# Gate and up of a second MLP by halves of the tokens, with seven matmuls in place of eight inside each product

## The chip, the cores and the metric

The kernel runs on one core of a Trainium2 chip. The core has a matrix engine (PE, with its weight loads, PEld), three engines for elementwise work (DVE, ACT, POOL) and a queue, SP, that issues all DMA transfers here. The engines run side by side, each through its own list of instructions in order, and wait for one another by semaphores. Matmul results go to PSUM[...]. The metric is the device time of one launch in microseconds, lower is better; differences are judged on the median.

## The reference

```python
x = x + 0.5 * ffn(layernorm(x))     # first MLP
x = x + attention(layernorm(x))     # 16 heads of 32, causal
x = x + 0.5 * ffn(layernorm(x))     # second MLP, same weights
# ffn:  inter = gelu(x @ Wg.T) * (x @ Wu.T);  out = inter @ Wd.T
```

x is 2048 tokens by 512 in float32. Wg and Wu are 4096 by 512, Wd is 512 by 4096; they come as 4-bit codes with scales. The first MLP decodes them and stores the decoded blocks in device memory; the second reads them back. All is float32.

## The kernel before

Both MLPs run in the function `ffn`. The 4096 inner rows are taken in 8 groups of 512, each in two halves (h = 0, 1) of 256. The 2048 tokens are two pairs of blocks (tp = 0, 1), 1024 tokens each. For a given group, h and tp, `slot` multiplies a 256 by 512 weight block by 512 by 1024 activations, for gate and then for up, in Strassen's way: each side is cut into 2 by 2 blocks, and seven products of sums of blocks stand for the eight products of blocks. A product is two matmuls of 128 by 128 weights with 512 columns (`product`, L313), which add in one PSUM bank. Each of the seven results is read out of PSUM once, by ACT (L352, L364) or DVE (L355 to L373), and the results are added up on the way; a sum of two results that both lie in SBUF is left to POOL (L367). ACT then does the gelu, in place (L333), and DVE the product of gate and up (L337), which gives `inter`.

The weight sums lie stored with the weights (made by the first MLP on POOL, L269 to L272). The token sums are made once, by `token_sums` (L293 to L296): for the first pair ahead of the first slot, t3 on POOL, for the second pair inside the first group.

The down projection (`down_pieces`) is in Strassen's form too: four sums of blocks of inter (L397 to L400, on DVE in the second MLP), then 14 pieces, each four matmuls of 256 columns (L412). Pieces read their bank by DVE (L420) or ACT (L434) into the residual x, and POOL adds intermediate results (L426). The 14 pieces of one tp are put one by one between the products of a later slot, so PE has other work while a bank is being read.

The program's order is written out by hand: each engine's instructions stand in the order in which this code emits them. The second MLP's first weights are fetched during the attention's sixth pass (`next_w`, L945), and the tokens of its first two blocks are normalized and transposed during the last pass. Blocks 2 and 3 are normalized inside the second MLP's first group. Later weights come as one transfer of 1792 KB for each half group, two buffers in turn, and wd as one transfer for each group (L539). PSUM has a pool of seven banks, `ps_one`, handed out in turn. The functions that the change touches, as the profile numbers their lines:

Of the kernel before, what the change touches and what calls it, by code (L numbers as in the profile page):

```python
# [2 lines left out]

# [6 lines left out]
F32 = mybir.dt.float32  # L10
# [4 lines left out]
AF = mybir.ActivationFunctionType  # L15
ALU = mybir.AluOpType
AX = mybir.AxisListType

P = 128
S = 2048  # L20
D = 512
H = 16
HD = 32
NT = S // P
NB = S // 512
NG = 8
NPAIR = H // 2
NQ = H // 4
EPS = 1e-5
# [5 lines left out]
def macaron_kernel(ctx: ExitStack, tc: tile.TileContext, x, packed, scales, wqk, bqk, wv, bv, wo, bo, out):  # L35
# [6 lines left out]
    nc = tc.nc  # L42
    PSUM = bass.MemoryType.PSUM

    const = ctx.enter_context(tc.tile_pool(name="const", bufs=1))
    res = ctx.enter_context(tc.tile_pool(name="res", bufs=1))
    small = ctx.enter_context(tc.tile_pool(name="small", bufs=2))
    store = ctx.enter_context(tc.tile_pool(name="store", bufs=1, space=bass.MemoryType.DRAM))
    ps_one = ctx.enter_context(tc.tile_pool(name="ps_one", bufs=7, space=PSUM))
# [5 lines left out]
    def weights(nm):  # L55
        return wts.tile([P, 7 * 512], F32, tag="w", name=nm)


    xpair = [res.tile([P, 2, D], F32, tag=f"x{t}", name=f"x{t}") for t in range(NT // 2)]
    xs = [xpair[t // 2][:, t % 2, :] for t in range(NT)]  # L60

    def load_x(tb):
# [5 lines left out]
    ident = const.tile([P, P], F32, tag="ident", name="ident")  # L68
    make_identity(nc, ident)
    eps = const.tile([P, 1], F32, tag="eps", name="eps")  # L70
    nc.gpsimd.memset(eps, EPS)
    expo = const.tile([P, 4], F32, tag="expo", name="expo")
    nc.gpsimd.memset(expo, -0.5)

    root = const.tile([P, 1], F32, tag="root", name="root")
# [2 lines left out]
    class Norm:  # L78
# [3 lines left out]
        def __init__(  # L82
            self, phase, tb, t_out, temp, on_act=(0, 1, 2, 3), on_pool=(), moments_on_act=False, power=False
        ):
            nm = f"{phase}_{tb}"
            tiles = [xs[4 * tb + i] for i in range(4)]

            def column(tag):
                return small.tile([P, 4], F32, tag=tag, name=f"{tag}_{nm}")

            rstd, nbias = column("rstd"), column("nbias")
# [27 lines left out]
            def scales():  # L119

                if power:
                    if moments_on_act:
                        nc.gpsimd.tensor_scalar(rstd, square, 1.0 / D, EPS, ALU.mult, ALU.add)
                    else:
                        nc.gpsimd.tensor_scalar(rstd, mv[:, :, 1], EPS, None, ALU.add)
                    nc.gpsimd.tensor_tensor(rstd, rstd, expo, ALU.pow)
                    if moments_on_act:
                        nc.gpsimd.tensor_tensor(nbias, total, rstd, ALU.mult)
                    elif on_act:
                        nc.gpsimd.tensor_scalar(nbias, mv[:, :, 0], -1.0, None, ALU.mult)  # L130
                        nc.gpsimd.tensor_tensor(nbias, nbias, rstd, ALU.mult)
                else:
                    nc.scalar.activation(rstd, mv[:, :, 1], AF.Sqrt, bias=eps)
                    nc.vector.reciprocal(rstd, rstd)
                    if on_act:
                        nc.vector.scalar_tensor_tensor(nbias, mv[:, :, 0], -1.0, rstd, ALU.mult, ALU.mult)
# [41 lines left out]
    def x_transposed(phase, tb):  # L178
        return res.tile([P, 4, 512], F32, tag=f"xT{tb}", name=f"xT_{phase}_{tb}")


    kept = {}

    def ffn(phase, finish, behind, loads, ready=(), first_w=None):
# [8 lines left out]
        with tc.tile_pool(name=f"w{phase}", bufs=1) as wp, tc.tile_pool(name=f"dq{phase}", bufs=1) as dq, tc.tile_pool(  # L193
# [283 lines left out]
            def run(steps):  # L477
                for f in steps:
                    f()
# [87 lines left out]
            for group in groups:  # L567
                run(group)

    def attention(xT, xT_f, wqk_wv, next_w):  # L570
        with tc.tile_pool(name="aw", bufs=1) as aw, tc.tile_pool(name="qk", bufs=1) as qkp, tc.tile_pool(
            name="pp", bufs=3
# [15 lines left out]
                out=mask_f, in_=mask_f, compare_op=ALU.is_ge, fill=MASKED, base=0, pattern=[[-1, P]], channel_multiplier=1  # L588
# [87 lines left out]
            later, divisions = [], {}  # L676
# [235 lines left out]
            qk, v = project_qk(0), project_v(0)  # L912
# [29 lines left out]
            for p in range(NPAIR):  # L942
                if p in refill:
                    nc.sync.dma_start(out=wqk_sb, in_=wqk[refill[p]])
                if p == 5:  # L945
                    next_w()
                fills = plan[p]() if p in plan else [[] for _ in range(NB)]
                if p == 4:
                    for piece in project_v(1)[:2]:
# [21 lines left out]
                n = 0  # L971
                for steps in attend(p, 2 if p + 1 == NPAIR else 1):
# [4 lines left out]
                    other = next(ahead, None)  # L977
# [30 lines left out]
    xT_a, xT_f, early = [], [], {}  # L1008
# [26 lines left out]
        nc.sync.dma_start(out=bv_sb, in_=bv.partition_broadcast(P))  # L1035

    def load_first():
        early["ffn"] = weights("w_2_0_0")
        nc.sync.dma_start(out=early["ffn"], in_=kept[0, 0])

    ffn(1, lambda *_: None, norms_behind, load_qkv)
    attention(xT_a, xT_f, early["qkv"], load_first)

    def store_out(t, half, x_):

        rows = out[t * P : (t + 2) * P, half * 256 : half * 256 + 256]
        nc.sync.dma_start(out=rows.rearrange("(j p) n -> p j n", p=P), in_=x_)

    ffn(2, store_out, lambda temp: [], lambda: None, xT_f, early["ffn"])


# [62 lines left out]
```

## Time and profile before

| | us |
|---|---|
| median of 3 runs | 3267.97 (3267.74 to 3269.58) |
| the profiled execution, its own time | 3267.61 |
| its span, first to last instruction | 3265.8 |
| PE, DVE, POOL, ACT busy | 3236.0, 1887.5, 1130.4, 873.4 |
| second MLP, first matmul to last instruction | 2099.3 to 3265.8 |
| one group of it (2851.18 to 2995.66) | 144.48 |

The span leaves out what lies around the program. A busy share says how long an engine had work, not that the work was needed then. In lists of groups, the columns are line, engine, operation, output and inputs with their shapes, count, then busy us and mean ns of one, then idle time of the engine before them and what ended it. A line's own view gives the shortest, median and longest duration in ns. A timeline line starts with its start and its duration in us. A float32 matmul shows as two PE records, so a product of two 512-column matmuls is four records.

### The profile page before, as it was taken

The numbers are of one execution on the slowest core, as the hardware profiler recorded it, in microseconds if no ns is written. First come the engines' busy times: TensorE is split into PE (matmuls) and PEld (weight loads), VectorE is DVE, ScalarE is ACT, GpSimd is POOL, SyncE is SP. The second block draws the span as 40 slices with busy tenths as digits, with TensorE's granted clock in tenths as the row PEclk, the third lists the DMA queues.
The fourth block names the chain that finished last, engine by engine and source line by source line (L and its number), as shares of the span: only waits on it lengthen the run. The fifth ranks groups of instructions, "written<-read, shape, count | busy, mean of one in ns | idle before, by whom it ended". The sixth has DMA issues, their size and how long they took to land.

```text
span 3265.8 us, 34006 instructions
## 1 busy us (share of the span) xinstructions
PE 3236.0 (99%) x12656; PEld 1720.2 (53%) x12656; DVE 1887.5 (58%) x2918; ACT 873.4 (27%) x1848; POOL 1130.4 (35%) x1339
## 2 busy tenths in 40 slices
PE   7999999999999999999999999999999999999999
PEld 3556565655656565333344333356556565655556
DVE  6666666666666555575654675555455445445545
ACT  4111111111111131464544555531111111111111
POOL 3546364555546341332212223213122221313222
PEclk9999999999999999999999999999999999999999
DMA  4111111111111100000000000101010101101101
GB/s 142 65 71 42 66 71 48 65 65 71 42 65 69 48 17 7 9 12 6 13 5 6 30 19 9 49 23 45 23 68 23 45 23 45 46 23 47 44 23 52
DMA packets 42054, 134.14 MB, mean 41 GB/s; under 512 B 5864, under 2 KB 26344, under 8 KB 35360
## 3 DMA queue, kind: packets, MB, share of 16 engines
q1 hardware_dynamic: 41888, 131.96, 11.0%
q8 instruction: 100, 1.64, 0.2%
q14 instruction: 66, 0.54, 0.1%
HBM read 81.91 MB, written 48.46 MB: 40 GB/s over the span
## 4 chain that ended last, share of the span: by engine, by line
PE 95%; ACT 2%; DVE 1%; POOL 1%; issue 1%; DMA 0%; SPq 0%; POOLq 0%; DVEq 0%; ACTq 0%
PE po L412 24%; PE pu L313 23%; PE pg L313 23%; PE av L779 8%; PE pm L714 6%; PE pqk L625 4%; PE ps L840 2%; PE pv L642 2%; PE pp L664 2%; PE ps L849 1%; ACT pt L872 1%; PE pt_f L153 0%; ACT both L788 0%; DVE parts L729 0%; PE pt_a L153 0%
## 5 line engine op out<-in xcount | busy, mean ns | idle before, releaser
L412 PE MATMUL po<-wd,inter 128*128 128x256 f32 x2048 | 482.2, 379 | 0.0
L313 PE MATMUL pg<-xT_f,w 128*128 128x512 f32 x1024 | 478.0, 595 | 0.4 <-ACT u L352 0.4
L313 PE MATMUL pu<-xT_f,w 128*128 128x512 f32 x1024 | 476.0, 592 | 0.0
L412 PEld LDWEIGHTS po<-wd,inter 128*128 128x128 f32 x2048 | 389.0, 190 | 155.2 <-issue 109.5
L729 DVE TENSOR_REDUCE parts<-pm 128x1 f32<-128x512 f32 (+3 forms) x640 | 370.5, 608 | 149.6 <-PE pm L714 135.6
L367 POOL TENSOR_TENSOR u<-u,u 128x512 f32<-128x512 f32 x128 | 162.9, 1272 | 839.4 <-ACT u L364 839.4
L426 POOL TENSOR_TENSOR x<-x,d 128x512 f32<-128x512 f32 x248 | 323.5, 1315 | 333.2 <-DVE d L420 164.8
L412 PE MATMUL po<-wd,s 128*128 128x256 f32 x1536 | 362.4, 379 | 0.0
L313 PE MATMUL pg<-xsum,w 128*128 128x512 f32 x768 | 356.7, 593 | 0.0
L313 PE MATMUL pu<-xsum,w 128*128 128x512 f32 x768 | 355.3, 592 | 0.0
L412 PEld LDWEIGHTS po<-wd,s 128*128 128x128 f32 x1536 | 291.4, 190 | 116.2 <-issue 82.8
L714 PE MATMUL pm<-kT,qT 32*128 32x512 f32 (+3 forms) x1280 | 334.3, 574 | 0.1
L872 ACT ACTIVATE pt<-ps 128x512 f32<-128x512 f32 (+3 forms) x576 | 271.8, 532 | 130.9 <-PE ps L849 130.0
L779 PE MATMUL av<-pt,vaug 128*64 128x512 f32 (+3 forms) x1280 | 299.7, 552 | 2.8 <-ACT both L788 2.3
L313 PEld LDWEIGHTS pg<-xT_f,w 128*128 128x128 f32 x1024 | 195.2, 191 | 194.3 <-issue 179.4
L313 PEld LDWEIGHTS pu<-xT_f,w 128*128 128x128 f32 x1024 | 194.3, 190 | 191.8 <-issue 183.2
L849 PE MATMUL ps<-qT,kT 32*128 32x512 f32 (+3 forms) x1280 | 277.9, 533 | 0.0
L313 PEld LDWEIGHTS pu<-xsum,w 128*128 128x128 f32 x768 | 145.8, 190 | 144.3 <-issue 139.0
L313 PEld LDWEIGHTS pg<-xsum,w 128*128 128x128 f32 x768 | 145.7, 190 | 142.5 <-issue 137.6
L420 DVE SCALAR_TENSOR_TENSOR d<-po,d 128x512 f32<-128x512 f32 x192 | 132.1, 688 | 107.4 <-PE po L412 106.5
L420 DVE SCALAR_TENSOR_TENSOR x<-po,x 128x512 f32<-128x512 f32 x192 | 131.8, 687 | 102.4 <-ACT d L434 69.7
L866 POOL TENSOR_SCALAR_AFFINE_SELECT pt<-pt 128x256 f32<-128x256 f32 x128 | 52.0, 406 | 396.1 <-ACT pt L865 395.8
(136 smaller groups left out, 3436.0 us busy)
## 6 DMA issues: line engine op xcount, KB each, us to landing
kept<-wd SPq DMA_DIRECT2D x8, 1792.0 KB
wd<-kept SPq DMA_DIRECT2D x8, 1792.0 KB
x<-in_x SPq DMA_DIRECT2D x16, 256.0 KB
pk<-in_gate_codes SPq DMA_DIRECT2D x16, 256.0 KB
sc<-in_gate_scales SPq DMA_DIRECT2D x32, 128.0 KB
pk<-in_up_codes SPq DMA_DIRECT2D x16, 256.0 KB
sc<-in_up_scales SPq DMA_DIRECT2D x32, 128.0 KB
pk<-in_down_codes SPq DMA_DIRECT2D x16, 256.0 KB
```

The costliest lines, as they stand in the source:

```text
L313: nc.tensor.matmul(ps, lhsT=a[:, j, :], rhs=b[:, j, :], start=(j == 0), stop=(j == 1))
L367: nc.gpsimd.tensor_tensor(u4, u4, u2, ALU.add)
L412: nc.tensor.matmul(ps[:, j, :], lhsT=a[i][:, k, bass.ts(2 * q + j, P)], rhs=b[i][:, k, :], start=(k == 0), stop=(k == 1),)
L420: stt(dst, ps, 0.5, other, ALU.mult, ALU.add)
L426: adder.tensor_tensor(dst, dst, other, ALU.add)
L625: nc.tensor.matmul(ps, lhsT=w[:, j, k, :], rhs=xT[tb][:, k, :], start=(k == 0), stop=(k == 3))
L642: nc.tensor.matmul(ps[:, i, :], lhsT=xT[t // 4][:, k, (t % 4) * P : (t % 4 + 1) * P], rhs=wv_sb[:, k, bass.ts(half, 256)], start=(k == 0), ...
L714: nc.tensor.matmul(ps[a][:, :n], lhsT=q[r, bass.ts(4 * g + i, P)], rhs=k[r, kb * 512 : kb * 512 + n], start=True, stop=not on_pe,)
L729: nc.vector.tensor_reduce(parts[:, a, i, kb : kb + 1], ps[a][:, :n], AX.X, ALU.max)
L779: nc.tensor.matmul(av[64 * a : 64 * a + 64, off:], lhsT=vaug[:, c, p % 4, HD * a : HD * a + 2 * HD], rhs=pt[:, a, off:], start=(c == 0), s ...
L849: nc.tensor.matmul(ps[a][:, off:], lhsT=k[r, bass.ts(c, P)], rhs=q[r, g * 512 + off : (g + 1) * 512], start=False, stop=True,)
L872: nc.scalar.activation(pt[:, a, plain:], ps[a][:, plain:], AF.Exp, scale=scale)
```

## The change

The second MLP leaves `ffn` and gets a function of its own, `second_ffn`; the first MLP stays.

- It goes through all eight groups with the first 1024 tokens, and then again with the other 1024. The rows of x of the later tokens are written to device memory (`away`) at its start. They are read back one block of 128 rows at a time for their normalization (the class `Later`: moments in the first half, then normalize on ACT, transpose on PE and copy on ACT around the border of the halves), and once more as the residual after the first half's last stores.
- A *problem* is one of the seven outer products of one group and h, now for gate and up together: 2 by 2 blocks of 128 by 128 weights against 2 by 2 blocks of 128 by 256 tokens. Its eight block products are replaced by seven, again in Strassen's way. Two problems form a *pair*, and share a PSUM bank, half of it each.
- Of the seven inner results some add up in PSUM: bank d takes products 1, 6, 7 and 4 in turn, and is read after each; f takes 5 and 3; e takes 2. ACT does four reads and DVE three (`pair`). The seven outer results are added one pair later, in SBUF (`recombine`): on DVE, and two of seven on POOL.
- The inner weight sums are made on POOL for each pair, two pairs ahead (`weight_sums`), from blocks that SP fetches four pairs ahead. The inner token sums are made on DVE, once in each half (`Tokens.inner`).
- Seven pairs are a group. The 14 down pieces of a group run during the next group's seven pairs, two in each; its four down sums stand in the second of these.
- Step numbers in `hooks` are the products of a pair: what stands at step k is emitted after the k-th.

```diff
-    xpair = [res.tile([P, 2, D], F32, tag=f"x{t}", name=f"x{t}") for t in range(NT // 2)]
+    xquad = [res.tile([P, 4, D], F32, tag=f"xq{t}", name=f"xq{t}") for t in range(NT // 4)]
+    xpair = [xquad[t // 2][:, 2 * (t % 2) : 2 * (t % 2) + 2, :] for t in range(NT // 2)]
...
+    problems = [(g, h, i) for g in range(NG) for h in range(2) for i in (1, 2, 6, 7, 5, 4, 3)]
+    NP = len(problems) // 2
...
+    def pair_of(n):
+        return problems[2 * (n % NP) : 2 * (n % NP) + 2]
...
+    def fetch(slot, pair):
+        for k, (g, h, i) in enumerate(pair):
+            place = {1: 0, 5: 1, 2: 2, 4: 3, 7: 4, 6: 5, 3: 6}[i]
+            nc.sync.dma_start(
+                out=slot[:, k, 0:4, :].rearrange("p (m c) n -> p m (c n)", m=2),
+                in_=kept[g, h].rearrange("p (m i c n) -> p i m (c n)", m=2, i=7, c=2)[:, place],
+            )
+    def weight_sums(slot):
+        a11, a12, a21, a22, s3, s2, s4 = [slot[:, :, y, :] for y in range(7)]
+        eng = nc.gpsimd
+        eng.tensor_tensor(s3, a11, a21, ALU.subtract)
+        eng.tensor_tensor(s2, a22, s3, ALU.subtract)
+        eng.tensor_tensor(a21, a21, a22, ALU.add)
+        eng.tensor_tensor(s4, a12, s2, ALU.subtract)
...
+    def second_ffn(finish, ready, slots):
...
+            away = store.tile([P, 2, 4 * D], F32, tag="away", name="away")
+            for q in range(2):
+                nc.sync.dma_start(out=away[:, q, :], in_=xquad[2 + q].rearrange("p t n -> p (t n)"))
+            residual = [xquad[0], xquad[1]]
...
+                def outer(self, first):
+                    b11, b21, b12, b22, t3, t2, t4 = [self.operand(x) for x in range(7)]
+                    return [
+                        lambda: first.tensor_tensor(t3, b22, b12, ALU.subtract),
+                        lambda: tt(t2, t3, b11, ALU.add),
+                        lambda: tt(b12, b12, b11, ALU.subtract),
+                        lambda: tt(t4, b21, t2, ALU.subtract),
+                    ]
...
+                def inner(self, t):
+                    n = 2 if t < 3 else 1
+                    v = (self.b1, self.b2, self.ts, self.t4)[t][:, : 2 * n, :].rearrange("p (x c) n -> p x c n", c=2)
+                    b11, b21 = [v[:, :, c, :256] for c in range(2)]
+                    b12, b22 = [v[:, :, c, 256:] for c in range(2)]
+                    t3, t2, t4 = [self.ys[:, 2 * t : 2 * t + n, k, :] for k in range(3)]
+                    t1 = b12 if t > 0 else self.t4[:, 2, :].rearrange("p (x n) -> p x n", x=2)
+                    return [
+                        lambda: tt(t3, b22, b12, ALU.subtract),
+                        lambda: tt(t1, b12, b11, ALU.subtract),
+                        lambda: tt(t2, t3, b11, ALU.add),
+                        lambda: tt(t4, b21, t2, ALU.subtract),
+                    ]
...
+            def pair(n, tokens, pieces, hooks):
...
+                fb = [tokens.factors(i) for _, _, i in pair_of(n)]
...
+                def product(ps, y, first=False):
+                    for k in range(2):
+                        nc.tensor.matmul(
+                            ps[:, k, :], lhsT=fa[k][y], rhs=fb[k][y], start=first and k == 0, stop=True,
+                            skip_group_check=True,
...
+                order = (1, 5, 2, 6, "a", 7, 3, "b", 4) if pieces else (1, 5, 6, 2, 7, 3, 4)
+                step = 0
+                for y in order:
+                    if y in ("a", "b"):
+                        for piece in pieces[y == "b"]:
+                            piece()
+                        continue
+                    if y == 1:
+                        d = bank("d")
+                        product(d, 1, True)
+                        u1 = taken("u1")
+                        nc.scalar.copy(u1, d)
+                    elif y == 5:
+                        f = bank("f")
+                        product(f, 5, True)
+                        u5 = taken("u5")
+                        nc.scalar.copy(u5, f)
+                    elif y == 2:
+                        e = bank("e")
+                        product(e, 2, True)
+                        tt(o[:, :, 0, :256], e, u1, ALU.add)
+                    elif y == 6:
+                        product(d, 6)
+                        u2 = taken("u2")
+                        nc.scalar.copy(u2, d)
+                    elif y == 7:
+                        product(d, 7)
+                        tt(o[:, :, 1, 256:], d, u5, ALU.add)
+                    elif y == 3:
+                        product(f, 3)
+                        tt(o[:, :, 0, 256:], f, u2, ALU.add)
+                    else:
+                        product(d, 4)
+                        nc.scalar.copy(o[:, :, 1, :256], d)
+                    for s in hooks.get(step, ()):
+                        s()
+                    step += 1
...
+            def recombine(n):
...
+                for g, h, i in pair_of(n):
+                    o = {j: outs.get((half, g, h, j)) for j in range(1, 8)}
+                    def add(dst, other, eng=nc.vector):
+                        sums.append(lambda: eng.tensor_tensor(dst, dst, other, ALU.add))
...
+                    def done(row, second, t, g=g, h=h):
+                        gelus.append(lambda: nc.scalar.activation(t[:, 0, :], t[:, 0, :], AF.Gelu_apprx_tanh))
...
+                        def gate():
...
+                            tt(inter[key][:, row, :], t[:, 0, :], t[:, 1, :], ALU.mult)
...
+                    if i == 2:
+                        add(o[2], o[1])
+                        done(0, 0, o[2])
+                    elif i == 6:
+                        add(o[6], o[1])
+                    elif i == 7:
+                        add(o[7], o[6], nc.gpsimd)
+                    elif i == 5:
+                        add(o[6], o[5], nc.gpsimd)
+                    elif i == 4:
+                        add(o[4], o[7])
+                        add(o[7], o[5])
+                        done(1, 0, o[4])
+                        done(1, 1, o[7])
+                    elif i == 3:
+                        add(o[3], o[6])
+                        done(0, 1, o[3])
+                return sums, gelus, gated
...
+                sums = [
+                    lambda: tt(s3, block(0, 0), block(0, 1), ALU.subtract),
+                    lambda: tt(block(0, 1), block(0, 1), block(1, 1), ALU.add),
+                    lambda: tt(s2, block(0, 1), block(0, 0), ALU.subtract),
+                    lambda: tt(s4, block(1, 0), s2, ALU.subtract),
+                ]
...
+                    a = {3: s4, 6: s2, 7: s3}[i] if i in (3, 6, 7) else block(i in (2, 4), i in (4, 5))
+                    ps = ps_one.tile([P, 2, 256], F32, tag="one", name=f"po{i}_{nm}")
+                    for j in range(2):
+                        for k in range(2):
+                            nc.tensor.matmul(
+                                ps[:, j, :], lhsT=a[:, k, bass.ts(2 * q + j, P)], rhs=wd[:, PLACE[i], k, :],
+                                start=(k == 0), stop=(k == 1),
+                            )
...
+                    if q == 1 and (half, g) != (1, NG - 1):
+                        load_wd((g + 1) % NG, i)
...
+                order = [(i, q) for i in (1, 2, 4) for q in range(2)] + [(i, q) for q in range(2) for i in (6, 5, 7, 3)]
+                return sums, [lambda i=i, q=q: piece(i, q) for i, q in order]
...
+            t3, t2, t1, t4 = tokens.outer(nc.gpsimd)
+            first, second, third, fourth = [tokens.inner(t) for t in range(4)]
+            for f in [t3] + first[:2]:
+                f()
+            at(0, 0, 0, *first[2:])
+            at(0, 0, 1, t2, t4)
+            at(0, 0, 2, *third[:2])
+            at(0, 0, 3, *third[2:])
+            at(0, 0, 4, t1)
+            at(0, 0, 6, *second[:1])
+            at(0, 1, 0, *second[1:])
+            at(0, 1, 2, *fourth)
...
+            at(0, 53, 5, call(later.load, 0), call(later.load, 1))
+            at(0, 53, 6, call(later.normalize, 0))
+            where = [(0, 54, 1), (0, 54, 4), (0, 55, 0), (0, 55, 3), (1, 0, 0), (1, 0, 2), (1, 0, 4), (1, 0, 6)]
+            for i, place in enumerate(where):
+                at(*place, call(later.transpose, i))
+                if i + 2 < 8:
+                    at(*place, call(later.load, i + 2))
+                if i + 1 < 8:
+                    at(*place, call(later.normalize, i + 1))
...
+            at(0, 55, 5, *first[:2])
+            at(0, 55, 6, *first[2:])
+            at(1, 0, 6, t3, t2, t4, *third)
+            at(1, 1, 0, t1)
+            at(1, 1, 2, *second)
+            at(1, 1, 5, *fourth)
...
+            for n in range(2 * NP + 1):
+                mine = {k: hooks.pop((n, k), []) for k in range(7)}
+                sums, gelus, gated = recombine(n - 1) if n else ([], [], [])
+                mine[1] = sums + mine[1]
+                mine[4] = gelus + mine[4]
+                mine[6] = gated + mine[6]
+                if n == 2 * NP:
+                    last, steps = pieces, mine[1] + mine[4] + mine[6] + down_sums
+                    for piece in last[:2]:
+                        piece()
+                    for f in steps[: -len(down_sums)]:
+                        f()
+                    for f, piece in zip(down_sums, last[2:6]):
+                        piece()
+                        f()
+                    for piece in last[6:]:
+                        piece()
+                    break
+                if n + 2 < 2 * NP:
+                    mine[3].append(call(weight_sums, slot(n + 2)))
+                if n + 4 < 2 * NP:
+                    mine[6].append(call(fetch, slot(n + 4), pair_of(n + 4)))
+                due = n % 7
+                take = 2 if pieces else 0
+                if n >= NP and n < NP + 7:
+                    take = 2 if due in (0, 1, 3, 4, 5, 6) else 0
+                if due == 1 and pieces:
+                    for k, f in enumerate(down_sums):
+                        (mine[k] if n != NP + 1 else mine[6]).append(f)
+                pair(n, tokens, [[pieces.pop(0)] for _ in range(take)], mine)
+                if n == NP:
+                    for _ in range(2):
+                        pieces.pop(0)()
+                if n == NP + 6:
+                    for q in range(2):
+                        residual[q] = res.tile([P, 4, D], F32, tag=f"xq{q}", name=f"xq_second_{q}")
+                        nc.sync.dma_start(out=residual[q].rearrange("p t n -> p (t n)"), in_=away[:, q, :])
+                if due == 6:
+                    assert not pieces
+                    down_sums, pieces = down(n // NP, n % NP // 7)
...
+                if p in (5, 6):
+                    next_w[p - 5]()
...
-        early["ffn"] = weights("w_2_0_0")
-        nc.sync.dma_start(out=early["ffn"], in_=kept[0, 0])
+        early["ffn"] = weights("ring_0")
+        for n in range(2):
+            fetch(ring_slot(early["ffn"], n), pair_of(n))
+    def sums_first():
+        for n in range(2):
+            weight_sums(ring_slot(early["ffn"], n))
```

Left out are, among others, the tail of `down`'s `piece`, which reads the banks as before, most of `Later` and of `Tokens`, and the allocation of tiles. In `done(row, second, t)` the gelu is queued for ACT and the product with inter for DVE; `weight_sums`, `Tokens.outer` and `Tokens.inner` are four sums each.

## The prediction

> **What bounds the kernel now.** I read the page's busy shares first, then the sums of each engine over one group of the second MLP, then the chain of waits at the group's two ends.
>
> ```profile
> PE 3236.0 (99%) x12656; PEld 1720.2 (53%) x12656; DVE 1887.5 (58%) x2918; ACT 873.4 (27%) x1848; POOL 1130.4 (35%) x1339
> ```
>
> ```profile
> 2851.18:2995.66 144.48, 144.48 (x450) 85.12 (x449) 72.17 (x97) 24.22 (x40) 36.29 (x28) 1.00 0.11 39
> ```
>
> ```profile
> 2178.57 1.73 PE po L412 x8
> ...
> 2851.18 12.02 PE pg L313 x28
> ...
> 2995.66 12.02 PE pg L313 x28
> ```
>
> The second line is a stretch of one group (columns: PE, PEld, DVE, ACT, POOL, clock): PE 144.48 of 144.48 us, at full clock; DVE works half of it, POOL a quarter. So each PE microsecond removed is gained, if DVE, ACT and POOL keep up. They are what has to be examined, because the change gives them more to do in less time. Their durations, from the groups of that stretch, from two lines' own views and from the timeline:
>
> ```profile
> L426 POOL TENSOR_TENSOR x<-x,d 128x512 f32<-128x512 f32 x16 | 21.1, 1327 | 28.1 <-DVE x L420 14.8 <-DVE d L420 13.3
> L367 POOL TENSOR_TENSOR u<-u,u 128x512 f32<-128x512 f32 x8 | 10.1, 1268 | 60.9 <-ACT u L364 60.9
> L420 DVE SCALAR_TENSOR_TENSOR d<-po,d 128x512 f32<-128x512 f32 x12 | 8.3, 689 | 7.6 <-PE po L412 7.6
> L399 DVE TENSOR_TENSOR s<-inter,inter 128x1024 f32<-128x1024 f32 x2 | 2.4, 1215 | 0.0
> L337 DVE TENSOR_TENSOR inter<-u,u x64: 691/692/1799, 2123.0 to 3235.4; 128x512 f32<-128x512 f32 x64
> L269 POOL TENSOR_TENSOR w<-w x32: 722/729/837, 18.9 to 1050.6; 128x256 f32<-128x256 f32 x32
> 2098.41 2.36 POOL L293 TENSOR_TENSOR xsum<-xT_f 128x1024 f32<-128x1024 f32 x1
> ```
>
> ```profile
> 3237.42 1.21 DVE L397 TENSOR_TENSOR s<-inter,inter 128x1024 f32<-128x1024 f32 x1
> 3238.66 2.18 DVE L398 TENSOR_TENSOR inter<-inter,inter 128x1024 f32<-128x1024 f32 x1
> 3240.88 1.22 DVE L399 TENSOR_TENSOR s<-inter,inter 128x1024 f32<-128x1024 f32 x1
> ...
> 3237.58 2.18 POOL L426 TENSOR_TENSOR x<-x,d 128x512 f32<-128x512 f32 x1 [1.23 <-DVE d L420]
> ```
>
> The last fence is the key. L398 takes 2.18 us beside a POOL sum, its sisters 1.21; the POOL sum, which takes 1.27 alone, takes 2.18 too. POOL ends at 3239.76 and DVE 1.08 later: they ran one after the other. DVE operations that read PSUM (L420) stay at 0.69 whatever POOL does.
>
> **What the Trainium skill says.** "SBUF — State Buffer", section "Who interferes with whom": a DVE instruction with two SBUF inputs contends with a GpSimd instruction that reads SBUF. The trace agrees, as just shown, and it alternates fairly when both queue. "PSUM — Partial Sum Buffer", section "The four PSUM rules": a partial sum may be read in the middle of an accumulation, and later matmuls without the first-flag add where the bank was written. No run here shows it yet; it makes the three-fold use of one bank possible, at no price but the wait for the reader.
>
> **The change, part by part.**
>
> *PE.* A 512-column float32 matmul is 12.02/14 = 0.8586 us. A group has 8 x 12.02 = 96.16 of these and 28 down pieces in the other 48.32, 1.726 a piece, 0.431 for a 256-column matmul. Afterwards a group of half the tokens has 7 pairs of problems; a pair is 14 matmuls of 256 columns, 6.04 us, and two pieces 3.45: 9.49. Seven pairs: 66.44. Two halves: 132.88 against 144.48; eight groups: **-92.8 us**. The eight transposes of the later tokens are in both.
>
> *Work of the others per seven pairs (66.4 us).* DVE: 33 PSUM operations x 0.69, 14 sums of 1024 x 1.215, 8 products x 0.69 = 45.3 (36.1 before in half a group). POOL: 28 weight sums x 0.73, 4 sums of 1024 x 2.36, 10 of 512 x 1.27 = 42.5 (18.1 before). ACT: 28 copies x 0.585, 8 gelus x 0.63, 4 scalings x 0.6 = 24. None is full. But POOL plus DVE's two-SBUF work (22.5) is 65 of 66.4, and these exclude each other, less some 0.14 us of fixed time in each.
>
> *Waits in a pair.* Order on PE: products 1, 5, 2, 6, a piece, 7, 3, a piece, 4. Bank d goes PE, ACT, PE, ACT, PE, DVE, PE. Copy of u1 takes 0.2 to see the end plus 0.585 plus about 0.1, inside the 1.72 of products 5 and 2; u2 has a piece, 1.73. DVE must read product 7 before product 4: product 3 and a piece give 2.59, so product 4 is due 8.63 into the pair. What is queued ahead of that read on DVE decides. I went through the seven pairs (0 to 6) by their queues:
>
> - Pair 6 has the most POOL work: 2 sums of 1024, 4 weight sums, 3 of 512, 12 us in 9.5. It runs some 4 us into pair 0.
> - Pair 0: DVE has three sums of 1024 (recombining the last problems), behind the ACT copy that lands 0.8 in. Each meets a POOL operation: waits 0.5, 1.2, 1.2. Then the reads of e, d, f: d at 8.3, just in time. Then three products with inter, each behind a weight sum (0.1, 0.6, 0.6): done 2.4 into pair 1.
> - Pair 1: four down sums and one recombining sum, 1.22 each, three of them behind weight sums (0.6 each; the weight sums of the next pair follow at once in POOL's queue, as only a landed transfer holds them). With e and a piece's read the queue comes to d at 11.4, ends 12.1. Product 4 starts 3.5 late. Where neighbours don't depend on one another, the trace starts the next 0.08 earlier; seven of these: 3.0.
> - Pairs 2 to 6: DVE has 4 to 8 us, d is read by 7.5. No stall.
>
> Without any lock wait the same queue is about on time (0 to 0.5 late). I take **3.0 us**; 14 of the 16 groups run so: **+42**. Bounds 7 and 90.
>
> *Head.* PE now starts the MLP at 2099.34 with x ready; token sums hide behind products 1 and 2. Afterwards product 5 needs an inner token sum, made after DVE's last residual add (2100.8) and one other inner sum: 2102.3 for 2100.2, +2.1. From 2102.2 DVE has six inner sums (0.69), two outer (1.22), e and d ahead of pair 0's product 4, 8.0 us: 2110.4 for 2106.7, +3.7. Pair 1 has seven more inner sums and a recombining sum ahead of its d, some behind the first weight sums: +5.5. Pairs 2 to 6 have no pieces: a copy's 0.9 against one product's 0.86 twice a pair, some 0.4 with d, and pair 3 about 1.8 for DVE's sums. Together **+15** (8 to 22).
>
> *Middle.* The later tokens' last transpose is at the end of the second half's first pair. After its copy (0.8) DVE has three outer sums and two inner ones, 5.0 us, ahead of the next pair's product 5; two extra pieces and product 1 cover 4.3: +1.5, and +1 at its product 4. Its down sums are put at its end, and the following pair has no pieces: its d waits for some 6. With lock waits **+10** (4 to 18).
>
> *Tail.* The third piece needs the last recombining, gelu and product, 5.3 to 7.5 after the end, with 3.45 of pieces as cover, and s2 is 1 late: **+5** (2 to 8).
>
> *Attention.* Eight weight sums, 8 x 0.81 with gaps, precede one mask on POOL, which ACT's exponentials wait for; two pending steps of some 2.8 us cover most: **+2** (0 to 5).
>
> *Transfers.* 512 KB a pair and 1.8 MB of down weights per seven, some 82 GB/s; the before trace reaches 447 in one slice. Fetches have over a pair of time; the residual rows sent away and back have ten pairs. On the SP queue a fetch waits for its slot's last matmul, and behind it down weights and stores, each with pairs to spare. Nothing, unless a fetch is over 12 us late; then POOL's weight sums wait, what is behind them on POOL, and PE. The wider exponent and the regrouped x tiles cost nothing: sizes and views.
>
> **Sum:** 3265.8 - 92.8 + 42 + 15 + 10 + 5 + 2 = 3247.0 of span. The profiled execution took 3267.61, the median of the runs is 3267.97, 2.2 above the span: **3249 us**.
>
> **Rivals.**
>
> - *DVE and POOL collide little* (POOL is early, or DVE slips into POOL's gaps between operations): the stall of pair 1 is 0.5, 7 us in all: 3214. For it: averages of 64 and 68%, and long gaps after POOL's sums in the trace of before. Against: POOL's work is bunched in pair 6, straight ahead of DVE's bunch. With the head and middle hidden too it ends at 3176, PE's own bound (1 in 20, counted here).
> - *The lock costs DVE more, and it ends slower*: in pairs 0 and 1, each of nine operations waits for a whole POOL operation (3 x 1.27, 6 x 0.73 = 8.2, against the 4.7 that count), so 6.5 us a group: 91 + 32 against 92.8, 3298 with the 2.2. It decides above (92.8 - 32)/14 = 4.3 us a group. For it: 65 of 66.4 us on one lock, and a POOL operation already waiting takes the lock in between. Against: in the trace a waiting DVE operation pays the remainder, 0.59 or 0.90 us, more often than the whole.
> - *The stall turns the clock down*: "TensorE: Matmul & The Clock Gate", section "What's actually happening", has the clock halved after an idle window of some 3.4 us. The before trace holds 1.00 here and has no such gaps. A stall of 3.0 is under it, a longer one is part of the slower case.
>
> **How the numbers follow.** Forecast case (stall 2 to 4.2 a group, 3233 to 3266): 0.43. Light: 0.30, 3176 to 3233. Slower: 0.27, 3266 to 3320. A difference within 0.2% (6.5 us) is about what cannot be told from none. Faster (under 3261.4): 0.30 + 0.36 = 0.66; within: 0.07 + 0.02 = 0.09; slower 0.25. Range for 8 in 10: 3205 to 3300; the forecast's own is 3233 to 3266.
>
> **What would show it.** PE matmuls of the second MLP sum to 93 us less; gaps of some 3 us once per seven pairs, before product 4 of the pair with the down sums, released by DVE's read of d; the recombining sums and down sums at 1.5 to 2.3 us in place of 1.2; POOL near 60% there; gaps of 10 us in all in the first two pairs and as many at the halves' border. The prediction is wrong if these gaps are absent (nearer 3200), if product 4 waits in other pairs too, or if product 6 or 7 waits for ACT.

## The result, and the profile after

The changed kernel takes **3266.75 us** (median; 3264.49 to 3268.28), the kernel before beside it 3267.82 (3266.02 to 3270.3). The ratio is 0.9996, 95% interval 0.9987 to 1.0004: no change that can be told from none. The profiled execution has a span of 3264.4 us, 1.4 less than before. The forecast was 3249, and a span of 3247.0. So nearly all of the 92.8 us taken from PE came back as something else.

The page's busy shares after:

```profile
PE 3175.8 (97%) x14000; PEld 1987.7 (61%) x14000; DVE 2201.7 (67%) x3078; ACT 1044.7 (32%) x2134; POOL 1700.0 (52%) x1785
```

PE has 60 us less to do but is idle for 88.6 us of the span where it was idle for 30. It lost 60 and not 93 of busy time mostly because some of its work now runs slower, as will be seen. DVE has 314 us more than before, POOL 570.

The same stretch as was read before, now two groups of seven pairs, each from product 4 of its pair 1 to the next group's (columns: length, then busy us of PE, PEld, DVE, ACT and POOL with the number of instructions, then the clock granted to PE, 1.00 full and 0.50 half, then the transfers' share and GB/s):

```profile
2469.56:2538.83 69.27, 66.74 (x308) 58.44 (x308) 54.91 (x56) 23.43 (x40) 54.21 (x43) 1.00 0.27 80
...
3041.31:3112.25 70.94, 68.43 (x308) 59.62 (x308) 54.46 (x56) 23.45 (x40) 54.17 (x43) 0.98 0.26 78
```

PE was busy for all of 144.48 us before; now 2.5 us are missing in each half. The two groups do the same work and stand still equally long, but the second is 1.67 us longer at a mean clock of 0.98. This pair of rows holds much of the answer. The waits of PE over the whole run say where it stands still (columns: total, times, longest):

```profile
PE d_f L705 <- DVE o_f L737: 47.8, 19, 4.3
...
PE av L1217 <- ACT both L1226: 7.2, 7, 5.5
PE f_f L705 <- DVE xT_f L668: 3.6, 2, 2.0
PE po_f L823 <- DVE inter_f L770: 1.6, 1, 1.6
```

The first is product 4, which waits for DVE to have read bank d after product 7. The gaps before it in pair 1 of the 14 regular groups (all but the first group of each half) are eleven of 2.5, two of 1.9 and one of 3.3, 34.6 us in all. DVE's queue in front of one of them, and two of POOL's operations beside it (start, duration; pair 0 starts at 3091.44, pair 1 at 3100.94):

```profile
3092.32 1.35 DVE L758 TENSOR_TENSOR o_f<-o_f,o_f 128x1024 f32<-128x1024 f32 x1 [0.85 <-ACT o_f L743]
3093.70 2.18 DVE L758 TENSOR_TENSOR o_f<-o_f 128x1024 f32<-128x1024 f32 x1
3095.80 2.29 DVE L758 TENSOR_TENSOR o_f<-o_f,o_f 128x1024 f32<-128x1024 f32 x1
...
3102.92 1.75 DVE L809 TENSOR_TENSOR s_f<-inter_f,inter_f 128x1024 f32<-128x1024 f32 x1
3104.59 1.75 DVE L758 TENSOR_TENSOR o_f<-o_f 128x1024 f32<-128x1024 f32 x1
3106.26 1.75 DVE L810 TENSOR_TENSOR inter_f<-inter_f,inter_f 128x1024 f32<-128x1024 f32 x1
...
3108.53 1.21 DVE L811 TENSOR_TENSOR s_f<-inter_f,inter_f 128x1024 f32<-128x1024 f32 x1
3109.77 1.23 DVE L812 TENSOR_TENSOR s_f<-inter_f,s_f 128x1024 f32<-128x1024 f32 x1
3111.52 0.68 DVE L737 TENSOR_TENSOR o_f<-d_f,u_f 128x512 f32<-128x512 f32 x1
...
3103.54 1.71 POOL L596 TENSOR_TENSOR ring<-ring 128x256 f32<-128x256 f32 x1
3105.21 1.71 POOL L597 TENSOR_TENSOR ring<-ring 128x256 f32<-128x256 f32 x1
```

The recombining sums and three sums in pair 1 take 1.35 to 2.29 us where the last two, which meet no POOL operation, take 1.2. The two weight sums of POOL take 1.71 there, and 0.73 alone. The read of d comes last, at 3111.52, and PE follows at its end:

```profile
3112.25 1.13 PE L705 MATMUL d_f<-ys_f,ring 128*128 128x256 f32 x4 [2.52 <-DVE o_f L737]
```

What the gap does to the clock shows when the trace is cut into equal windows of 3.413 us (columns as above). The first two rows are a gap in one group, the next two the gap just shown:

```profile
2608.29:2611.70 3.41, 1.94 (x9) 1.73 (x10) 3.36 (x7) 0.59 (x1) 1.92 (x2) 1.00 0.24 75
2611.70:2615.12 3.42, 3.42 (x18) 3.01 (x17) 2.62 (x2) 1.76 (x3) 2.26 (x2) 1.00 0.54 158
...
3110.05:3113.46 3.41, 1.21 (x6) 1.08 (x7) 3.41 (x6) 0.04 (x1) 1.27 (x1) 1.00 0.28 77
3113.46:3116.88 3.42, 3.42 (x10) 2.71 (x9) 2.69 (x2) 1.32 (x3) 2.18 (x2) 0.50 0.48 153
```

Both gaps are 2.5 us. Where PE was busy for 1.94 of the window, the next runs 18 matmuls at full clock; where it was busy for 1.21, the next runs 10 at half clock, and 1.7 us are lost. This befell 8 of the 14 gaps: the one of 3.3 us, neither of the two of 1.9, and seven of the eleven of 2.5. Among those eleven the difference is only how a gap lies across the windows' borders. The windows form a fixed grid: the stretches at half clock begin at 2256.72, 2328.40, 2400.08 and so on to 3113.46, which is 21, 42 and 251 times 3.413 us after the first.

Ahead of the second MLP, in the attention's seventh pass, there is one more idle place. By time on POOL and PE, with the stretch in which PE goes on:

```profile
1924.56 0.73 POOL L594 TENSOR_TENSOR ring<-ring 128x256 f32<-128x256 f32 x1
...
1930.27 0.41 POOL L1304 TENSOR_SCALAR_AFFINE_SELECT pt<-pt 128x256 f32<-128x256 f32 x1
...
1932.89 1.97 PE L1217 MATMUL av<-pt,vaug 128*64 128x512 f32 x4 [5.46 <-ACT both L1226]
...
1932.45:1939.28 6.83, 6.39 (x28) 1.88 (x28) 1.39 (x6) 2.27 (x9) 1.82 (x7) 0.50 0.01 1
```

The mask of L1304 stands behind eight weight sums on POOL, 1924.56 to 1930.3, and PE waits for 5.46 us, then runs at half clock for two windows.

### The profile page after: what moved, and what is told of

The parts are those of the page before. It is cut to its first block, busy times and chain, and to the rows that moved or that the text cites. A ratio compares the mean times of both kernels' runs of the same rounds, so it can differ in the third digit from the quotient of the medians.

```text
span 3264.4 us, 39140 instructions
## 1 busy us (share of the span) xinstructions
PE 3175.8 (97%) x14000; PEld 1987.7 (61%) x14000; DVE 2201.7 (67%) x3078; ACT 1044.7 (32%) x2134; POOL 1700.0 (52%) x1785
## 4 chain that ended last, share of the span: by engine, by line
PE 84%; DVE 9%; issue 3%; ACT 2%; POOL 2%; DMA 0%; SPq 0%; DVEq 0%; POOLq 0%; ACTq 0%
PE po L414 12%; PE pu L315 11%; PE pg L315 11%; PE d_f L705 9%; PE po_f L823 9%; PE av L1217 8%; PE pm L1152 6%; PE f_f L705 4%; PE pqk L1063 4%; PE ps L1278 2%; PE e_f L705 2%; PE pv L1080 2%; PE pp L1102 1%; PE ps L1287 1%; DVE o_f L758 1%
## 5 line engine op out<-in xcount | busy, mean ns | idle before, releaser
L705 PE MATMUL d_f<-ys_f,ring 128*128 128x256 f32 x1344 | 353.2, 386 | 48.8 <-DVE o_f L737 47.8
L705 PEld LDWEIGHTS d_f<-ys_f,ring 128*128 128x128 f32 x1344 | 254.6, 192 | 95.8 <-DVE o_f L737 57.7
L758 DVE TENSOR_TENSOR o_f<-o_f,o_f 128x1024 f32<-128x1024 f32 x128 | 251.4, 1974 | 34.7 <-ACT o_f L743 32.5
L1304 POOL TENSOR_SCALAR_AFFINE_SELECT pt<-pt 128x256 f32<-128x256 f32 x128 | 52.3, 408 | 396.4 <-ACT pt L1303 396.1
L823 PE MATMUL po_f<-wd_f,inter_f 128*128 128x256 f32 x1024 | 241.2, 379 | 1.6 <-DVE inter_f L770 1.6
L414 PEld LDWEIGHTS po<-wd,inter 128*128 128x128 f32 x1024 | 194.4, 190 | 77.5 <-issue 55.7
L414 PE MATMUL po<-wd,inter 128*128 128x256 f32 x1024 | 241.1, 379 | 0.0
L315 PE MATMUL pg<-xT_f,w 128*128 128x512 f32 x512 | 240.8, 598 | 0.0
L705 PE MATMUL f_f<-xT_f,ring 128*128 128x256 f32 x896 | 237.1, 388 | 3.6 <-DVE xT_f L668 3.6
L315 PE MATMUL pu<-xT_f,w 128*128 128x512 f32 x512 | 238.0, 592 | 0.0
L823 PEld LDWEIGHTS po_f<-wd_f,inter_f 128*128 128x128 f32 x1024 | 194.4, 190 | 28.3 <-DVE inter_f L770 2.0
```

The costliest lines, as they stand in the source:

```text
L315: nc.tensor.matmul(ps, lhsT=a[:, j, :], rhs=b[:, j, :], start=(j == 0), stop=(j == 1))
L414: nc.tensor.matmul(ps[:, j, :], lhsT=a[i][:, k, bass.ts(2 * q + j, P)], rhs=b[i][:, k, :], start=(k == 0), stop=(k == 1),)
L705: nc.tensor.matmul(ps[:, k, :], lhsT=fa[k][y], rhs=fb[k][y], start=first and k == 0, stop=True, skip_group_check=True,)
L758: sums.append(lambda: eng.tensor_tensor(dst, dst, other, ALU.add))
L823: nc.tensor.matmul(ps[:, j, :], lhsT=a[:, k, bass.ts(2 * q + j, P)], rhs=wd[:, PLACE[i], k, :], start=(k == 0), stop=(k == 1),)
```

## The experiments

My theory after this reading: the cost of the change is the stall in pair 1, made by POOL's weight sums holding DVE up on sums that stand ahead of the read of d, and a clock that is halved behind many of these stalls. Rivals: the read of d would be late wherever the down sums stand, because DVE's work as a whole is behind; and the halved clock is a matter of some other cause than PE's idle time.

**e1_spread_first_sums**: the eight weight sums of the first two pairs go into the attention's seventh pass one by one, after steps that have no mask, in place of all ahead of its masks.

```diff
-                if p in (5, 6):
-                    next_w[p - 5]()
+                if p == 5:
+                    next_w[0]()
...
+                if p == 6:
+                    for k, f in zip((24, 25, 26, 27, 34, 35, 36, 37), next_w[1]()):
+                        extra.setdefault(k, []).append(f)
```

> The eight first weight sums stand one by one after eight steps of the seventh attention pass that have no mask, in place of all at once ahead of its masks. Theory (POOL's queue: the mask waits for eight sums, PE for the mask, and the idle window then halves the clock for 6.8 us): the start of the second MLP, 2107.6 in the changed kernel, comes back by 8 us to within 1 of 2099.3, and the time falls by 7 to 9 us to 3258.5. Rival (the 8 us come from the smaller fetches of the pass before, or from POOL being busier at all): the second MLP still starts at 2105 or later and the time stays above 3264.

Measured: 3257.26 us (3255.85 to 3258.21), ratio to before 0.9968 (0.9956 to 0.998); against the changed kernel's median 9.5 us less. Waits of PE in it, over the whole run:

```profile
PE d_f L715 <- DVE o_f L747: 47.7, 19, 4.3
...
PE av L1227 <- ACT both L1236: 2.3, 8, 0.5
```

The 5.5-us gap is gone, the 47.7 of the second MLP are untouched. The second MLP starts at 2099.88 in place of 2107.57, so 7.7 us came back ahead of it, as the theory had it; by the medians it is 9.5, a little more than was expected. Of this, 4.9 us are standing still (7.2 less 2.3), and the two windows at half clock behind the gap, 3.4 us, are gone, though one new one stands at 2071.21. The remainder isn't taken apart.

**e2_down_sums_later**: the four down sums stand one pair later, among the same steps of pair 2.

```diff
-                if due == 1 and pieces:
+                if n == NP + 1:
+                    mine[6] += down_sums
+                elif due == 2 and pieces and n != NP + 2:
                     for k, f in enumerate(down_sums):
-                        (mine[k] if n != NP + 1 else mine[6]).append(f)
+                        mine[k].append(f)
```

> The four down sums of 14 groups stand in the third of the seven pairs in place of the second; nothing else moves. Theory (DVE's queue in the first two pairs is too long[...] so the read of d is late there and nowhere else): the 14 gaps before product 4, 34.6 us, and the eight half-clock windows behind them, 1.7 us each, go: 3219, range 3213 to 3230, and pairs two and three last 9.5 us each. Rival (DVE and POOL are full on average[...]): the gap only moves to the third pair or later and the time stays at 3255 to 3268.

Measured: 3267.67 us (3265.83 to 3270.07), ratio 0.9999 (0.999 to 1.0007). The expectation missed by 49 us: nothing was gained. Waits of PE:

```profile
PE d_f L705 <- DVE o_f L737: 48.1, 19, 4.3
```

The same total in as many waits: from the starts of the product matmuls, pair 2 now takes 12.3 us, and its gaps are of 2.5. DVE and POOL in one pair 2 (it starts at 3113.05), by time:

```profile
3118.68 2.77 DVE L811 TENSOR_TENSOR s_f<-inter_f,inter_f 128x1024 f32<-128x1024 f32 x1
3121.48 1.63 DVE L812 TENSOR_TENSOR s_f<-inter_f,s_f 128x1024 f32<-128x1024 f32 x1
3123.64 0.68 DVE L737 TENSOR_TENSOR o_f<-d_f,u_f 128x512 f32<-128x512 f32 x1
```

```profile
3117.10 3.27 POOL L758 TENSOR_TENSOR o_f<-o_f 128x1024 f32<-128x1024 f32 x1 [2.30 <-DVE o_f L758]
```

By itself this speaks for the rival that the place doesn't matter. But POOL's own sum of 1024 runs in pair 2 and collides with the down sums there. I had looked at where DVE had room, and not at what POOL does at that moment. (The down sum that starts at 3118.68 ends 1.08 after POOL's sum, which ends at 3120.37: it waits for the remainder of POOL's operation.) The down sums ahead of the read of d are enough to make it late in this pair too; whether another place would do stays open here.

**e3_no_weight_sums**: the weight sums are left out from the fifth pair of the second MLP on, so the products there use factors that are not sums, and the output isn't the reference's.

```diff
-                if n + 2 < 2 * NP:
+                if n + 2 < 4:
                     mine[3].append(call(weight_sums, slot(n + 2)))
```

> Leaves out POOL's inner weight sums of all but the first four pairs of the second MLP (old sums are used, so the output is not the reference's); DVE, ACT and PE have the same instructions. Theory[...]: without them DVE's nine two-input operations of the first two pairs wait 1 us in all in place of 5, the 14 gaps are under 0.5 us, the clock stays up, and the time is near 3215 (3205 to 3228). Rival (DVE's queue is too long in itself): gaps of 2 us and more stay, and the time is above 3255.

Measured: 3212.35 us (3211.35 to 3214.74), ratio 0.9832 (0.9817 to 0.9846). A stretch of one group, and the waits of PE:

```profile
2977.34:3043.82 66.48, 66.48 (x309) 58.52 (x308) 47.89 (x56) 23.10 (x40) 24.14 (x14) 1.00 0.28 84
```

```profile
PE d_f L705 <- DVE o_f L737: 12.5, 5, 3.8
```

All 14 gaps are gone, PE is busy throughout at full clock, and DVE's 56 instructions take 47.89 us instead of 54.5 though none was removed from DVE. So DVE is late because of POOL's weight sums. (In the changed kernel their 28 cost POOL 30 us a group, 1.07 each, where one alone takes 0.73: POOL waits as well.) The rival that DVE by itself is behind has fallen.

**e4_filler_in_gap**: four matmuls of 256 columns, 1.73 us, whose result nobody reads, go in front of product 4 in pair 1, so PE is busy in most of the gap, and nothing else is moved.

```diff
                     else:
+                        if n % 7 == 1 and pieces and n != NP + 1:
+                            idle = ps_acc.tile([P, 512], F32, tag="acc", name=f"idle_{nm}")
+                            for j in range(4):
+                                nc.tensor.matmul(idle[:, :256], lhsT=fa[0][1], rhs=fb[0][1], start=True, stop=True)
                         product(d, 4)
```

> Adds four matmuls of 256 columns, 1.73 us of PE, into an unused bank ahead of product 4 of the 14 late pairs, where PE idles 1.9 to 3.3 us. Their result is used by nothing. Theory (an idle share of about 0.57 of a clock window halves the clock of the next window, at 1.7 us each): PE's gap there shrinks to 0.8, none of the eight half-clock windows behind these gaps comes, and the time falls by 12 to 15 us to 3253. Rival (the half clock has another cause, or costs nothing because PE is waiting anyway): no change, 3265 to 3268, or slower by the added work.

Measured: 3253.02 us (3252.39 to 3254.12), ratio 0.9956 (0.9941 to 0.997): with more work on PE, 13.7 us less than the changed kernel. The stretch of a group:

```profile
3053.25:3122.50 69.25, 68.47 (x318) 59.96 (x317) 54.90 (x56) 23.42 (x41) 54.16 (x43) 1.00 0.27 80
```

DVE's and POOL's sums are as before, the late pair still takes 12.27 us, and no window behind these gaps runs at half clock. So the clock is PE's own idle time's doing, and it cost 13.7, as 8 x 1.7 = 13.6 says.

**e5_down_sums_behind_d**: the down sums two by two at the ends of pair 1 and pair 2, behind the read of d.

```diff
-                if due == 1 and pieces:
-                    for k, f in enumerate(down_sums):
-                        (mine[k] if n != NP + 1 else mine[6]).append(f)
+                if n == NP + 1:
+                    mine[6] += down_sums
+                elif due in (1, 2) and pieces and n != NP + 2:
+                    for k in range(2):
+                        mine[5 + k].append(down_sums[2 * due - 2 + k])
```

> The four down sums of 14 groups stand behind the reads of d and f, two in the second pair and two in the third, in place of all four ahead of the read of d in the second pair (the third, in the run before). Theory, as mended after that run (a pair's PE waits for what DVE has queued ahead of its read of d, and four down sums[...] are too many in any one pair): no gap over 0.5 us before product 4 in these groups, a group of 66.5 us in place of 69 to 71, no half-clock window behind them; 3219 (3213 to 3225). Rival ([...]some pair must be late): gaps of 2 us come back at another pair and the time stays above 3250.

Measured: 3216.57 us (3213.83 to 3218.51), ratio 0.9844 (0.983 to 0.9859). A stretch of one group:

```profile
2900.00:2966.50 66.50, 66.50 (x310) 58.68 (x309) 53.94 (x56) 23.22 (x40) 55.32 (x43) 1.00 0.28 84
```

DVE and POOL collide as much as in the changed kernel (53.94 and 55.32 us busy), and it costs nothing: what waits is no longer ahead of something that PE needs. The edit does two things at once, though: the sums stand behind the read, and there are two of them in a pair in place of four. Whether either alone would do wasn't run. The whole price of the stall is 3266.75 - 3216.57 = 50.2 us: 34.6 of gaps, 13.7 of clock, and 2 left, about what PE's busy time itself grows around a gap at full clock (66.74 against 66.50, 14 x 0.24 = 3.4; its reason isn't shown).

**e15_both_moves** is the edits of e1 and e5 together, nothing else.

> The run before and the spread first weight sums together. Theory (the two are independent): 3219 less 9.5, 3209.5 (3204 to 3216). Rival (part of the first gain is given back when the second MLP starts earlier, at its head): above 3216.

Measured: 3208.71 us (3207.15 to 3209.31), ratio 0.9821 (0.9805 to 0.9838). The two gains add up but for 1.6 us: 3266.75 less 9.5 and 50.2 would be 3207.1. The head of the second MLP takes 59.75 us here and 58.77 in the changed kernel, with three windows at half clock in place of two.

**e6_middle_and_fillers** adds to it the same split of the down sums at the border of the halves, and four idle matmuls ahead of product 4 in the first two pairs and in the second half's pair 1.

```diff
+                        if n in (0, 1, NP + 1):
...
                 if n == NP + 1:
-                    mine[6] += down_sums
-                elif due in (1, 2) and pieces and n != NP + 2:
+                    mine[6] += down_sums[:2]
+                elif n == NP + 2 or due in (1, 2) and pieces:
```

> As the run before; the down sums at the border of the halves are split over two pairs as well, and four unused matmuls stand ahead of product 4 in the first two pairs and in the second pair of the second half. Theory: three half-clock windows fewer (3.4 us at the head, 3.4 at the border) and 2.5 us less waiting in the pair after: 3200 (3196 to 3205). Rival (the fillers delay the late products as much as the clock gave): 3206 to 3212.

Measured: **3203.03 us** (3201.43 to 3203.28), ratio 0.9802 (0.9788 to 0.9817), 2.0% faster than before and the fastest of all. Its page and its waits of PE:

```profile
PE 3157.2 (99%) x14024; PEld 1980.7 (62%) x14024; DVE 2191.7 (68%) x3078; ACT 1041.5 (33%) x2134; POOL 1716.7 (54%) x1785
```

```profile
PE d_f L715 <- DVE o_f L747: 6.8, 4, 2.6
```

PE is at 99% of its span again. From the starts of the product matmuls, the head went from 59.75 us in e15_both_moves to 57.26, where only the idle matmuls act: two of its three windows at half clock are gone. The border's seven pairs went from 80.40 to 78.08, with one such window in place of two; there the two edits aren't told apart.

## Why the prediction was wrong

The forecast was faster by 19 us, and the time came out 17.8 above it, unchanged; the range of 3205 to 3300 holds it. Step by step, in us of span:

| step | predicted | measured | from |
|---|---|---|---|
| PE's work | -92.8 | -92.2 | groups without gaps take 66.48 for 66.44: 8 x 144.48 - 16 x 66.48 |
| stall in pair 1, 14 groups: the gaps | +42 | +34.6 | 14 gaps in the trace |
| the same: half clock behind 8 of them | 0 | +13.7 | e4_filler_in_gap |
| the same: PE slower around the gap | 0 | +2 to +3.4 | remainder of e5; stretches |
| head | +15 | +16.5 | 58.77 for seven pairs of 6.04 without pieces; 3.4 of it clock |
| middle | +10 | +12.3 | 80.65 - 66.48 - 1.9, four transposes in these pairs; 3.4 of it clock |
| tail | +5 | +3.3 | 27.5 for 24.2 |
| attention | +2 | +8.2 | start of the second MLP 2107.57 for 2099.34; 9.5 by the medians of e1 |
| sum | -18.8 | -1.6 to -0.2 | span: -1.4 |

*The stall* was right in mechanism, place and releaser: once in seven pairs, before product 4 of the pair with the down sums, released by DVE's read of d, from sums that wait for POOL. The single waits in pair 0 were predicted as 0.5, 1.2 and 1.2 and came as 0.1, 1.0 and 1.1. e3_no_weight_sums shows POOL's weight sums as the cause, e5 that their collisions with DVE cost nothing once the down sums are split and stand behind the read. Its size, 3.0, was 2.5. POOL was busy for 54.17 us of a group's 70.94, 76% where some 60 was said, because it waits as DVE does.

*The step that failed* is the rival "The stall turns the clock down", which was set aside because a stall of 3.0 us is under an idle window of some 3.4. The Trainium skill's page "TensorE: Matmul & The Clock Gate", section "What's actually happening", has a free-running window of 3413 ns, whose length and fixed grid these traces show too, and a clock that drops after an idle one. In this last point the measurement decides otherwise: the window need not be idle. In the 14 gaps, a window of 3.41 us with 1.46 us or less of PE work was followed by half clock, and one with 1.51 or more wasn't, so some 1.95 us of idle time within one window were enough, which a gap of 2.5 us has or hasn't by its place on the grid. Measured in its place: 13.7 us behind these gaps (e4_filler_in_gap), where the sum had 0. Counted with the head, the border and the attention, clock took some 24 us (8 x 1.7 + 3 x 3.4). Without it the time would have been near 3243 (3266.75 - 24), inside the forecast's own range of 3233 to 3266.

*Attention* is the second term, mis-sized: the eight sums took 5.7 us (1924.56 to 1930.3) for the 6.5 of 8 x 0.81, but the cover was wrong. Two pending steps were to hide most of it; PE stood still for 5.46. ACT waited for the mask from 1925.14 and PE had work until 1927.43, so the cover was 2.3 us, not 5.6; half clock behind the gap, 3.4 us, came on top.

*Head* came near by luck: f waited 2.05 for 2.1 and product 4 of pair 0 3.85 for 3.7, as worked out, but product 4 of pair 1 waited 2.11 where 5.5 was said, and two windows at half clock, which were put at nothing, made up the 3.4. *Tail* was within its range. *Middle* is close by wrong parts: product 5 waited 1.53 for 1.5, but product 4 of the same pair 4.32 where 1 was said, the following pair 1.30 where some 6 was said, and the clock took 3.4. Why its DVE work ran late a pair sooner wasn't tested.

*The transfers*, put at nothing, cost nothing: the groups of e3 and e5 run without a gap of PE with the same transfers, 78 to 84 GB/s in a group. *The lock costs DVE more*, the slower rival at 6.5 a group, was too dear: 2.5 us a group were lost in the gaps, and a waiting operation paid the remainder of POOL's operation, as in e2, not the whole. *DVE and POOL collide little* was wrong as a statement on the engines, yet its time, 3214, is nearly what e5 gives by removing the consequence only.

## What to carry to other kernels

Two engines whose averages over the run leave a third of the time and more free can still stall the one that sets the end, if one of them is held up ahead of a read that frees that engine's buffer: move the work that can wait behind the read (here two sums in each of two pairs, 50 us) rather than make it less, and look at what the other engine does in the place where you put it. Price a stall of TensorE with what it does to the clock, not by its length alone: look for stretches at half clock behind each gap, and count how the gap falls on the windows. When work is put ahead of something on a shared queue, ask whether what is to hide it is still undone at that moment.

## What the runs showed of the hardware

- In the second MLP the clock of a window of the 3.413-us grid went with PE's work in the window before it. Multiply PE's busy share of that window by the clock that it ran at itself: in the traces of the changed kernel and of all seven experiments, half clock followed every window up to 0.426, and full clock every one from 0.429 (the ends of matmuls are modelled in the profile, so the last digit is not to be trusted). The own clock counts: at the border in the changed kernel the window from 2690.21 ran at half clock with PE busy for 2.45 us (0.72 x 0.5 = 0.36), and the next stayed at half clock; the window from 2256.72, also at half clock, had 3.35 us (0.98 x 0.5 = 0.49), and full clock followed. In the attention, whose matmuls have other shapes, the border lies elsewhere: in e1_spread_first_sums the window from 2067.80, at full clock, had 1.60 us, a share of 0.47, and half clock followed. This is a regularity of these traces; nothing here tells how it is made. The two nearest to it in the changed kernel's gaps, each with the window behind it:

```profile
2396.66:2400.08 3.42, 1.46 (x7) 1.30 (x8) 3.42 (x6) 0.29 (x1) 1.45 (x2) 1.00 0.29 77
2400.08:2403.49 3.41, 3.41 (x10) 2.70 (x9) 2.44 (x2) 1.47 (x3) 2.25 (x2) 0.50 0.53 154
...
2970.10:2973.52 3.42, 1.51 (x7) 1.35 (x8) 3.42 (x6) 0.34 (x1) 1.50 (x2) 1.00 0.33 77
2973.52:2976.93 3.41, 3.41 (x18) 3.00 (x17) 2.99 (x3) 1.66 (x4) 2.25 (x2) 1.00 0.55 159
```

- 1.73 us of idle matmuls in a gap of 2.5 make the kernel 13.7 us faster over 14 gaps.
- POOL pays for the collisions as DVE does: its sum of 128x512 went from 1.27 alone to a mean of 1.57 (L838 in a group), its sum of 128x1024 from 2.36 to 3.27 in e2, while DVE reads of PSUM stayed at 0.68 to 0.69 in the group.
- Bank d was read three times in the middle of its accumulation in each pair, which the Trainium skill's page "PSUM — Partial Sum Buffer", section "The four PSUM rules", says the hardware allows. It cost PE nothing where the reader was in time: in the group of e5 PE was busy for 66.50 of 66.50 us.
